# Attention layer and gated graph steps on one core: another start-up, another order of loads, and new ranks for the planner

## The chip, the cores and the metric

The kernel runs on one core of a Trainium2 chip. The time is the device time of one execution in microseconds (us). TensorE multiplies matrices, VectorE (DVE) and ScalarE (ACT) do elementwise work, GpSimd (POOL) does small arithmetic and can issue DMAs, SyncE (SP) issues most DMAs. Each engine works through its own instructions strictly in order, and waits on semaphores for the others.

## The reference

The input x is 16 batches of 1024 nodes by 128 features; adj is a symmetric 0/1 matrix of 1024 by 1024 with a full diagonal. Two layers are computed, each as layernorm(x + layer(x)).

```python
# layer 0: attention over graph edges
h = x @ others_weight
u1, u2 = h @ a1, h @ a2              # a1, a2: the two halves of att_weight
e = u1[:, idx1] + u2[:, idx2]        # pairs of nodes
e = where(e >= 0, e, 0.1 * e)
att = softmax(where(adj > 0, e, -9e15), axis=1)
out = einsum('bik,bkl->bil', att, h) + x @ self_weight

# layer 1: five gated steps
m_in = m_out = einsum('nm,bmd->bnd', adj, h)
av = concatenate([m_in, m_out])
u3 = h @ u3_w.T + u3_b
z = sigmoid(av @ w3_w.T + w3_b + u3)
r = sigmoid(av @ w4_w.T + w4_b + u3)
hv = tanh(av @ w5_w.T + w5_b + (r * h) @ u5_w.T + u5_b)
h = (1 - z) * h + z * hv
```

The pair indices are such that in the first half of the columns a logit depends on two neighbouring nodes of the second index alone, and in the other half on the row alone. So the attention of a batch needs one vector of 1024 logits (u1 + u2 of the same node, exponentiated) spread over all partitions, called pb, and one number for each row, called q.

## The kernel before

**A planner orders everything.** The kernel does not emit instructions as its code runs. Each piece of work is put into a `Plan` (L36 to L134) with its engine, a length in ns, a rank, the tiles that it reads and writes, and the function that emits it. `order()` plays the plan through in model time: whenever an engine is free, the ready piece with the lowest rank whose buffers are free is started. A piece that needs another engine's result becomes ready after a lag (`LAG`, L47: 150 ns after VectorE, 170 after ScalarE, 2400 after a DMA), for TensorE after VectorE or ScalarE with another `CARE` = 400 ns (L45, L125), and lengths on these two are multiplied by 1.1. The order in which the pieces were started becomes the fixed program of each engine. So ranks and model lengths set the order of all work, and nothing of it can change while the kernel runs.

**Ranks.** A step s of batch b has the rank 10 * (b // 2) + 4.2 * s (`rank_of`, L314), layer 0 of a batch has `rank0` (L317), and the table D (L303, L304) holds an offset for every kind of work: m for copying a message bank out, pu and u for the product with u3, pr and pz for the gates, r for the product r * h, pv and hv for the candidate, h for the update, tr for the turn of the new state, o and ln for the end of a batch, l1 to l8 for the parts of layer 0. Batches come in pairs q = b // 2. Pairs are staggered, so that attention of later batches runs beside the gated steps of earlier ones. `LATER` (L29) puts the last batch behind its partner in the last three steps.

**Work on TensorE.** In layer 0, h of a batch (ph, L668), the two attention halves (po, L631 through `product`), the self products (px, L935 and L949, with wsi = self weight + identity). In layer 1, the messages: a state is split into a high and a low part (`split`, L613), and multiplied with the adjacency matrix, in most steps by a scheme with seven instead of eight quarter products (L1130 to L1180), which needs the sums T1 to T4 of quarters of adj (`sums_of_adj`, L499, 16 operations on VectorE). Then per half of a batch the gates: L1199, L1209 twice, L1225, L1226.

**The start.** `early_loads` (L340) issues the first loads: x of batch 0 in two halves, the weights for the logits, adj in eight blocks of 256 rows by 512 columns (`adj_half`; first the four left ones, then the four right ones), the self weight, x of batch 1, then the w, u and bias loads, all of the latter on SyncE. `lands` (L372) tells the planner when each is there. The vector of logit weights is made by a transpose of att to columns (L409), a product with the transposed others_weight (pw, L398), and four small VectorE operations (wv_, L400). Its sum, broadcast over 128 columns (T_ws), is the weight of `spread_` (L744), whose product with x gives the logits of batch 0 on all partitions. `lrelu_` and `exp_` (L747, L753) turn them into pb. `adj_tables` (L473) copies adj into its rounded form, with the count of each row's right half. `z_` (L822) sums each row, `rz_` (L840) makes the reciprocals, `hi_` and `lo_` (L870, L876) scale and split h, and po follows. `ahead` (L444) makes the self products of batches 4 to 7 early (x halves in free r and z buffers, bank ps_ahead, L455) and stores them in DRAM.

**Filler.** `fill_` and `idle_` (L417 to L429) are matmuls and transposes of the identity on TensorE with no use for the result: two fills, and 60 pieces of two transposes at rank 9000, which the planner starts whenever TensorE has nothing else.

Of the kernel before, what the change touches and what calls it, by code (L numbers as in the profile page):

```python
# [9 lines left out]
F32 = mybir.dt.float32  # L10
# [15 lines left out]
LOW, HIGH = -20.0, 100.0  # L26
TINY = 1e-30
PLAIN = {(0, 0), (0, 1), (0, 2), (7, 2), (7, 3), (7, 4)}
LATER = 1.5  # L29
# [3 lines left out]
IDLE = 60  # L33


class Plan:  # L36
# [8 lines left out]
    CARE = 400  # L45
    SAME = {"PE": 0, "DVE": 60, "ACT": 60, "POOL": 60, "SP": 2500, "DMA": 0}
    LAG = {"PE": 250, "DVE": 150, "ACT": 170, "POOL": 200, "SP": 2500, "DMA": 2400}  # L47

    def __init__(self, slots):
        self.slots = dict(slots)  # L50
        self.ops = []
        self.lag = {}
        self.writer, self.readers = {}, {}

# [19 lines left out]
    def order(self):  # L74
# [14 lines left out]
        while events:  # L89
# [13 lines left out]
            while more:  # L103
                more = False
                for engine, queue in ready.items():
# [3 lines left out]
                    while queue:  # L109
# [3 lines left out]
                        if all(free[t[0]] > 0 for t in new):  # L113
# [3 lines left out]
                            started.append(i)  # L117
                            busy[engine] = more = True
# [19 lines left out]
def kernel(  # L138
# [72 lines left out]
    att2 = const.tile([P, 2], F32, tag="att2", name="att2")  # L211
# [3 lines left out]
    bad = const.tile([P, 5], F32, tag="bad", name="bad")  # L215
    flag = const.tile([1, 1], I32, tag="flag", name="flag")

    def exact(pools):
# [84 lines left out]
        D = dict(m=-0.8, pu=1.4, u=0.8, pr=0.8, pz=1.2, r=1.7, pv=1.0, z=1.3, hv=-0.4, h=1.2, tr=1.6, o=6.6, ln=2.9)  # L303
        D.update(out=4.4, l1=-9, l2=-4, l3=-2, l4=-4, l5=-7, l6=-1.5, l7=-1, l8=-2)  # L304

# [8 lines left out]
        def rank_of(b, s):  # L314
            return 10 * (b // 2) + 4.2 * s + (LATER if b == B - 1 and plain(b // 2, s) else 0)

        def rank0(b):  # L317
            return 10 * (b // 2) - 1 * (1 - b % 2) + -1.0 - 6 * (b // 2 == 1)
# [7 lines left out]
        cols = {"wot": slice(0, 128), "ws": slice(128, 256), "w345": slice(256, 1024)}  # L326
# [13 lines left out]
        def early_loads():  # L340
            nc.sync.dma_start(T(x0)[:, HALF:N], x_t[0][:, HALF:N])
            nc.scalar.dma_start(T(x0)[:, 0:HALF], x_t[0][:, 0:HALF])
            nc.sync.dma_start(W("wot"), others_wt)
            nc.scalar.dma_start(T(ws)[0:2, P : 2 * P], att_w.rearrange("(t p) o -> t (p o)", p=P))
            nc.sync.dma_start(*adj_half(0, 0))
            nc.scalar.dma_start(wo[:, 0:P], others_w)
            nc.sync.dma_start(*adj_half(1, 0))
            nc.scalar.dma_start(*adj_half(2, 0))
            nc.sync.dma_start(*adj_half(3, 0))
            for k in range(NC // 2):  # L350
                nc.sync.dma_start(*adj_half(k, 1))
            nc.sync.dma_start(W("ws"), self_w)
            nc.sync.dma_start(T(("xt", 1)), x_t[1])
            for j, w in enumerate((w3_t, w4_t, w5_t)):
                nc.sync.dma_start(
                    W("w345")[:, 256 * j : 256 * (j + 1)].rearrange("p (t e) -> p t e", t=2),
                    w.rearrange("(t p) e -> p t e", p=P),
                )
            nc.sync.dma_start(u3, u3_t)
            nc.sync.dma_start(u5, u5_t)  # L360
            for j, v in enumerate((w3_b, w4_b, w5_b, u3_b, u5_b)):
                nc.sync.dma_start(T(ws)[j : j + 1, 2 * P : 3 * P], v.rearrange("(o p) -> o p", o=1))


        sp(
            6000,
# [5 lines left out]
        def lands(pieces, what):  # L372
            plan.add("DMA", 190 * pieces, -103, lambda: None, writes=what)

        lands(8, [(x0, 0), (x0, 1)])
        lands(1, [(boot, "wot"), (ws, "att")])
        lands(8, [(staged[0][0], 0)])
        lands(1, [(("wo",), 0)])
        for k in range(1, NC // 2):
            lands(8, [(staged[k][0], 0)])  # L380
        for k in range(NC // 2):
            lands(8, [(staged[k][1], 0)])
        lands(9, [(boot, "ws"), (("xt", 1), 0), (("xt", 1), 1)])
        lands(10, [(boot, "late"), (("uw",), 0), (ws, "b")])
# [7 lines left out]
        plan.add("POOL", 2000, -100, constants, writes=[(("ident",), 0), (("ones",), 0)])  # L392


        pw = ("ps", "g", "w")

        def pw_():
            nc.tensor.matmul(T(pw)[:, 0:2], W("wot"), att2, start=True, stop=True)  # L398

        def wv_():  # L400
            nc.vector.tensor_copy(wv, T(pw)[:, 0:2])
            nc.vector.tensor_copy(wo[:, P : P + 2], wv)
            nc.vector.tensor_tensor(wo[:, P + 2 : P + 3], wv[:, 0:1], wv[:, 1:2], ALU.add)
            nc.vector.tensor_copy(T(ws)[:, 0:P], wo[:, P + 2 : P + 3].to_broadcast([P, P]))

        pa = ("ps", "g", "a")
# [4 lines left out]
        pe(150, -101, lambda: column_(pa, slice(P, 2 * P), 2), reads=[(ws, "att"), (("ident",), 0)], writes=[(pa, 0)])  # L411
        dve(160, -101, lambda: nc.vector.tensor_copy(att2, T(pa)[:, 0:2]), reads=[(pa, 0)], writes=[(("att2",), 0)])
        pe(350, -100, pw_, reads=[(boot, "wot"), (("att2",), 0)], writes=[(pw, 0)])
        dve(600, -100, wv_, reads=[(pw, 0), (("wo",), 0)], writes=[(("wo",), 1), (ws, 0)])


# [27 lines left out]
        def ahead():  # L444
            dve(270, -8, self_, reads=[(boot, "ws"), (("ident",), 0)], writes=[(("wsi",), 0)])
            for b in AHEAD:
                d = ("PX", b)
                for e in range(2):
                    bank, px, x = ("ps", "ahead", b, e), ("m", "px", b, e), ("rz"[e], "x", b)
                    hs = slice(e * HALF, (e + 1) * HALF)  # L450
                    sp(450, -89, lambda x=x, b=b, hs=hs: nc.sync.dma_start(T(x), x_t[b][:, hs]), writes=[(x, "sent")], lag=0)
                    plan.add("DMA", 4 * 190, -101, lambda: None, reads=[(x, "sent")], writes=[(x, 0)])
# [5 lines left out]
                    act(A, -5.5, lambda bank=bank, px=px: nc.scalar.copy(T(px), T(bank)), reads=[(bank, 0)], writes=[(px, 0)])  # L458
# [8 lines left out]
        def own_weights():  # L467
            pb_ = ("ps", "g", "b")
            pe(150, -4.6, lambda: column_(pb_, slice(2 * P, 3 * P), 5), reads=[(ws, "b"), (("rz", 0), 1)], writes=[(pb_, 0)])
            dve(160, -4.3, lambda: nc.vector.tensor_copy(bias, T(pb_)[:, 0:5]), reads=[(pb_, 0)], writes=[(("bias",), 0)])  # L470
            dve(1000, -4.2, sums, reads=[(boot, "late"), (("bias",), 0), (("uw",), 0), (("rz", 0), 1)], writes=[(("wm",), 0)])

        def adj_tables(c):  # L473
            st = staged[c // 2]

            def left(copy):
                copy(adj[:, c, 0:HALF], T(st[0])[:, c % 2])

            def right():
                nc.scalar.activation(adj[:, c, HALF:N], T(st[1])[:, c % 2], AF.Identity, accum_out=cnt[:, c : c + 1])  # L480

            if c < 4:
                dve(420, -60, lambda: left(nc.vector.tensor_copy), reads=[(st[0], 0)], writes=[(("A",), c, 0)])
            else:
                act(A, -60, lambda: left(nc.scalar.copy), reads=[(st[0], 0)], writes=[(("A",), c, 0)])
            act(640, -50, right, reads=[(st[1], 0)], writes=[(("A",), c, 1)])
# [12 lines left out]
        def sums_of_adj(c):  # L499
# [17 lines left out]
            for n, (sum_, first) in enumerate(((t1, None), (t3, None), (t2, 0), (t4, 2))):  # L517
                more = [] if first is None else [(("tab",), c, first)]
                dve(V, 1 + c / 4, sum_, reads=[*y, *more], writes=[(("tab",), c, n)])
# [121 lines left out]
        def layer0(b):  # L641

            first = rank0(b) - (60 if b == 0 else 0)
            rank = first + D["l1"]
# [6 lines left out]
            if b in (2, 3):  # L651
                xt = ("hT", "x", b)
            q, zs, rz, hT = ("q", b), ("zs", b), ("rz", b), ("hT", b)
# [7 lines left out]
            for g in range(4):  # L661
# [18 lines left out]
                pe(460, rank, ph_, reads=[(xt, g // 2), (("wo",), 1)], writes=[(ph, 0), (hx, g, "place")])  # L680
# [55 lines left out]
            else:  # L736

                if b == 0:

                    for e in range(2):  # L740
# [14 lines left out]

                        pe(F, rank - 0.1, spread_, reads=[(xt, e), (ws, 0)], writes=[(pp, 0)])
                        dve(2 * V, rank - 0.1, lrelu_, reads=[(pp, 0)], writes=[(pb, e)])
                        act(A, rank - 0.1, exp_, reads=[(pb, e), (("ones",), 0)], writes=[(pb, e)])
# [34 lines left out]

            rank = first + D["l2"]

# [20 lines left out]
            rank = rank0(b) + D["l2"]  # L816
            junk = ("junk", b)
# [19 lines left out]
            for k in range(2 if b == 0 else 1):  # L837
                cs = slice(4 * k, 4 * k + 4) if b == 0 else slice(0, NC)

                def rz_(k=k, cs=cs):  # L840
# [3 lines left out]
                    if b == 0:  # L844
                        least = T(("rstd", "least"))[:, 0, k : k + 1]
                        nc.vector.tensor_reduce(least, w, AX.X, ALU.min)
                        nc.vector.tensor_scalar(bad[:, k : k + 1], least, 0.0, None, ALU.is_le)
                    nc.vector.tensor_scalar(w, w, TINY, None, ALU.max)
                    nc.vector.reciprocal(w, w)
                    nc.vector.tensor_tensor(T(rz)[:, 1, cs], w, T(q)[:, cs], ALU.mult)  # L850

# [6 lines left out]
                    writes=[(rz, k), (("bad",), k), (("rstd", "least"), k)] if b == 0 else [(rz, 0), (rz, 1)],  # L858
                )
            if b == 0:  # L860
                own_weights()
            rank = rank0(b) + D["l3"]
# [28 lines left out]
            rank = rank0(b) + D["l4"]  # L891
# [28 lines left out]
            px = ("xt", b, "px") if b in AHEAD else ("ps", "acc", b, "px")  # L920
            if b in AHEAD:
# [3 lines left out]
                    rank0(b) + D["l3"],  # L925
# [5 lines left out]
            else:  # L931
# [4 lines left out]
                    reads=[(xt, 0), (("wsi",), 0), (yT[1], "p")],  # L936
# [14 lines left out]
            begun = [(hl[1][0], c, 1) for c in range(4)]  # L951
# [21 lines left out]
            for g in range(2):  # L973
                rank = rank0(b) + D["l5"]
# [734 lines left out]
```

## Time and profile before

| | |
|---|---|
| time, median of 3 runs | 1455.69 us |
| lowest and highest | 1454.83 and 1457.84 us |
| span of the profiled execution | 1457.2 us |
| mean granted TensorE clock | 0.995 |
| last matmul starts | 1445.82 us |
| DMA moved | 174.20 MB, mean 120 GB/s |

The profiled execution's own total is not recorded beside its span; the span runs from its first to its last instruction. On the page, busy time is the union of an engine's instructions. PE is TensorE, PEld its weight loads. A row of the timeline gives start, length, engine, line, operation, output and inputs, count, and in brackets the idle time before it with what ended it.

### The profile page before, as it was taken

Reading aid. Unit: us, or ns where it says so; the run is one execution under the profiler, and the core shown is the slowest. Engines: PE = TensorE matmul, PEld = TensorE weight load, DVE = VectorE, ACT = ScalarE, POOL = GpSimd, SP = SyncE. Lnnn points to the kernel's source line nnn. Section 1 sums busy time; section 2 is a strip of 40 time slices with the busy share of each in tenths; the row PEclk is TensorE's granted clock in tenths of the full one; section 3 lists DMA queues with packets and bytes.
Section 4 is the critical chain, followed back from the end, with each engine's and each line's share of the span. In section 5 each row is a group of like instructions: output and inputs, shape, how many; then the busy total and the mean of one; then the engine's idle time right before and its main releaser. Section 6 shows DMA issues by size and latency. Waiting matters only on the chain.

```text
span 1457.2 us, 17798 instructions
## 1 busy us (share of the span) xinstructions
PE 1437.5 (99%) x5020; PEld 901.6 (62%) x5020; DVE 1161.3 (80%) x2753; ACT 897.1 (62%) x1792; POOL 194.8 (13%) x323
## 2 busy tenths in 40 slices
PE   8999999999999999999999999999999999999996
PEld 7766656666666666665666656666666666565663
DVE  5887879888899788878898778886989867866435
ACT  5657565666666666756667566566665666654544
POOL 0311001012110120110201112001210112000201
PEclk9999999999999999999999999999999999999998
DMA  7426134455345543445344553455433544223201
GB/s 252 136 58 210 48 102 139 120 174 160 88 137 146 152 132 103 135 130 145 110 116 116 148 148 96 116 142 170 118 84 99 163 139 122 80 58 87 73 0 31
DMA packets 188048, 174.20 MB, mean 120 GB/s; under 512 B 34255, under 2 KB 137382, under 8 KB 187942
## 3 DMA queue, kind: packets, MB, share of 16 engines
q1 hardware_dynamic: 182306, 156.28, 37.7%
q0 software_dynamic: 4800, 15.73, 3.2%
q8 instruction: 41, 0.67, 0.2%
q10 hardware_dynamic: 836, 0.98, 0.2%
q14 instruction: 65, 0.53, 0.1%
HBM read 95.68 MB, written 77.24 MB: 119 GB/s over the span
## 4 chain that ended last, share of the span: by engine, by line
PE 97%; DMA 2%; DVE 1%; ACT 0%; issue 0%; SPq 0%; POOL 0%; POOLq 0%; DVEq 0%; ACTq 0%
PE ps_acc_a L631 17%; PE ps_g_r L1209 9%; PE ps_g_r L1199 9%; PE gz L1209 9%; PE ps_g_v L1225 9%; PE ps_g_v L1226 9%; PE ps_acc_c L631 9%; PE ps_acc_po L631 8%; PE ps_acc L631 6%; PE gz L631 4%; PE ps_g_ph L668 2%; PE ps_acc_px L935 1%; PE ps_acc_po L949 1%; PE ps_t L581 1%; DMA blk_boot<-in_adj_dram 1%; DMA hT_boot<-in_L_gnn_w_w_dram 1%
## 5 line engine op out<-in xcount | busy, mean ns | idle before, releaser
L1225 PE MATMUL ps_g_v<-m,wm 128*128 128x512 f32 x320 | 163.5, 592 | 0.1
L1226 PE MATMUL ps_g_v<-r,u5h 128*128 128x512 f32 x320 | 163.4, 592 | 0.0
L1209 PE MATMUL ps_g_r<-m,wm 128*128 128x512 f32 x320 | 159.1, 592 | 1.1 <-ACT gz L1202 1.1
L1209 PE MATMUL gz<-m,wm 128*128 128x512 f32 x320 | 158.8, 592 | 0.0
L1199 PE MATMUL ps_g_r<-hT,u 128*128 128x512 f32 x320 | 153.1, 592 | 0.0
L1219 DVE SCALAR_TENSOR_TENSOR r<-r,hT 128x512 f32<-128x512 f32 x160 | 108.7, 685 | 54.0 <-ACT r L1212 53.4
L1212 ACT ACTIVATE r<-ps_g_r,bh 128x512 f32<-128x512 f32 x160 | 109.4, 687 | 63.6 <-PE ps_g_r L1209 61.1
L631 PE MATMUL ps_acc_a<-tab,blk_s 128*128 128x512 f32 x544 | 147.0, 412 | 0.0
L1234 DVE TENSOR_TENSOR hv<-hv,hT 128x512 f32<-128x512 f32 x160 | 109.6, 686 | 45.1 <-ACT hv L1231 44.6
L631 PE MATMUL ps_acc_po<-adj,blk 128*128 128x512 f32 x512 | 138.1, 417 | 0.0
L1212 ACT ACTIVATE z<-gz,bh 128x512 f32<-128x512 f32 x160 | 109.3, 687 | 24.0 <-PE gz L1209 23.2
L631 PEld LDWEIGHTS ps_acc_a<-tab,blk_s 128*128 128x128 f32 x544 | 101.1, 188 | 32.6 <-issue 9.4
L631 PEld LDWEIGHTS ps_acc_po<-adj,blk 128*128 128x128 f32 x512 | 96.2, 189 | 33.6 <-issue 9.6
L1202 ACT COPY gz<-ps_g_r 128x512 f32<-128x512 f32 x160 | 91.1, 572 | 33.2 <-PE ps_g_r L1199 31.7
L1240 DVE SCALAR_TENSOR_TENSOR hT<-hv,hT 128x512 f32<-128x512 f32 x160 | 107.9, 678 | 1.4
L1237 DVE SCALAR_TENSOR_TENSOR hv<-z,hv 128x512 f32<-128x512 f32 x160 | 107.7, 677 | 1.4 <-ACT z L1212 0.5
L1226 PEld LDWEIGHTS ps_g_v<-r,u5h 128*128 128x128 f32 x320 | 60.6, 190 | 76.7 <-issue 64.2
L1209 PEld LDWEIGHTS gz<-m,wm 128*128 128x128 f32 x320 | 60.6, 190 | 76.5 <-issue 76.5
L631 PE MATMUL ps_acc<-adj,blk_h 128*128 128x512 f32 x384 | 101.5, 414 | 0.0
L533 POOL TENSOR_SCALAR rstd_y<-mv_y 128x4 f32<-128x4 f32 x32 | 12.7, 397 | 660.6 <-DVE mv_y L529 660.2
L623 DVE TENSOR_TENSOR blk_s<-G,blk_s 128x512 fp32r<-128x512 f32 x136 | 91.3, 682 | 12.0 <-ACT blk_s L619 11.6
L619 ACT CAST blk_s<-G 128x512 fp32r<-128x512 f32 x136 | 82.1, 618 | 29.1 <-DVE G L1093 26.2
(191 smaller groups left out, 2584.4 us busy)
## 6 DMA issues: line engine op xcount, KB each, us to landing
G<-X SPq DMA_DIRECT2D x140, 256.0 KB
X<-T SPq DMA_DIRECT2D x552, 64.0 KB
yd<-y POOLq DMA_DIRECT2D x32, 256.0 KB, 3.3
D_y<-T_y SPq DMA_DIRECT2D x112, 64.0 KB
F_y<-D_y SPq DMA_DIRECT2D x28, 256.0 KB
X<-y SPq DMA_DIRECT2D x28, 256.0 KB
D_b<-T_b SPq DMA_DIRECT2D x112, 64.0 KB
F_b<-D_b SPq DMA_DIRECT2D x28, 256.0 KB
```

Source lines behind the costliest of these rows:

```text
L623: lambda: nc.vector.tensor_tensor(half(1), src(), half(0), ALU.subtract),
L631: nc.tensor.matmul(T(bank), T(blk)[:, k, c, :], right(c), start=(first and i == 0), stop=(last and i == len(terms) - 1), skip_group_check= ...
L1199: nc.tensor.matmul(T(pr), u3, h(), start=True, stop=True)
L1202: nc.scalar.copy(T(pz), T(pr))
L1209: nc.tensor.matmul(T(p_), wm[:, j, :], T(m), start=False, stop=True, skip_group_check=True)
L1212: nc.scalar.activation(T(t), T(p_), AF.Tanh, bias=bh[:, j : j + 1], scale=0.5 * sg)
L1219: lambda r=r, h=h: nc.vector.scalar_tensor_tensor(T(r), T(r), 1.0, h(), ALU.add, ALU.mult),
L1225: nc.tensor.matmul(T(pv), wm[:, 2, :], T(m), start=True, stop=False)
L1226: nc.tensor.matmul(T(pv), u5h, T(r), start=False, stop=True)
L1234: nc.vector.tensor_tensor(T(hv), T(hv), h(), ALU.subtract)
L1237: nc.vector.scalar_tensor_tensor(T(hv), T(z), 1.0, T(hv), ALU.add, ALU.mult)
L1240: nc.vector.scalar_tensor_tensor(h(), T(hv), 0.5, h(), ALU.mult, ALU.add)
```

## The change

The vectors of logit weights are now made on VectorE, by multiplying others_weight with a broadcast copy of att and summing along the row. The blocks of adj are loaded in row order (left and right of one block of rows after each other). The w, u and bias loads are issued by GpSimd, behind a copy that reads the last block of adj. Of the second half of batch 0's logits, ScalarE makes two exponentials from the bank and VectorE takes the larger. Batch 0's px goes to a gz bank, and neither its px nor its second product waits for the earlier part of the batch. The check for a vanishing row sum moves out of the chain. The ranks of layer 0 have their own entries for batches 0 and 1. Nearly every offset of D, some lags and CARE change, and NUDGE adds a number to the rank of single steps and batches.

```diff
+MOST = math.exp(HIGH - SHIFT)
+LARGE = 0.999e30
-LATER = 1.5
+LATER = 0.75
+NUDGE = {(3, 2): -0.6, (3, 3): 0.3, (0, 1): -0.5, (1, 1): 0.45, (2, 3): -0.2, (3, 1): -1.2, (3, 0): 0.6, (0, 2): 0.25, (2, 2): -0.6, (1, 4): -1.2, (1, 3): 0.3, (0, 3): -0.6, (1, 2): -0.15, (4, 0): -0.1, (2, 0): 1.2, (2, 1): 0.05, (4, 4): -0.3, (2, 4): -0.15, (7, 3): -0.75, (5, 4): 1.2, (4, 3): 1.25, (6, 3): -1.5, (6, 4): -0.6, (8, 2): 0.15, 10: 0.05, (11, 3): -1.2, (11, 4): 0.3, (7, 2): 0.3, (8, 3): -0.6, (12, 3): -0.45, (13, 3): -0.9, (12, 0): 1.15, (10, 3): -0.35, (8, 4): 0.05, (12, 4): -0.3, (12, 1): -0.05, (11, 2): -0.15, 12: -0.05, (13, 4): 1.2, (13, 0): 1.2, (11, 1): 0.05, (12, 2): 0.15, (10, 4): 0.1, (15, 0): -0.6, (14, 2): -0.6}
...
-    CARE = 400
+    CARE = 250
...
-    LAG = {"PE": 250, "DVE": 150, "ACT": 170, "POOL": 200, "SP": 2500, "DMA": 2400}
+    LAG = {"PE": 250, "DVE": 330, "ACT": 80, "POOL": 200, "SP": 2500, "DMA": 3000}
...
-        D = dict(m=-0.8, pu=1.4, u=0.8, pr=0.8, pz=1.2, r=1.7, pv=1.0, z=1.3, hv=-0.4, h=1.2, tr=1.6, o=6.6, ln=2.9)
-        D.update(out=4.4, l1=-9, l2=-4, l3=-2, l4=-4, l5=-7, l6=-1.5, l7=-1, l8=-2)
+        D = dict(m=-0.05, pu=1.4, u=0.95, pr=0.55, pz=0.85, r=0.25, pv=1.05, z=1.3, hv=-0.7, h=1.2, tr=2.55, o=6.35, ln=2.5, out=4.4, l1=-9, l2=-4, l3=-2, l4=-5.5, l5=-7.25)
+        D.update(l6=-1.35, l7=-1, l8=-2, q=10, s=4.2, even=1, base=-1, q1=-6, b1=4, lz=-4, l1_0=-9, l2_0=-4, lz_0=-4, l3_0=-2, l4_0=-4, l5_0=-7, l6_0=-1.5, l7_0=-1, l8_0=-2)
+        D.update(l1_1=-10, l2_1=-9, lz_1=-4, l3_1=-2, l4_1=-4, l5_1=-7, l6_1=-1.5, l7_1=-1, l8_1=-2, tab=8, tabc=1, cl=-5.9, ca=-50, cr=-51, px=-3.5, own=-2, ownw=-4.6)
...
-            return 10 * (b // 2) + 4.2 * s + (LATER if b == B - 1 and plain(b // 2, s) else 0)
+            return D["q"] * (b // 2) + D["s"] * s + NUDGE.get((b, s), 0) + (LATER if b == B - 1 and plain(b // 2, s) else 0)
...
-            return 10 * (b // 2) - 1 * (1 - b % 2) + -1.0 - 6 * (b // 2 == 1)
+            return NUDGE.get(b, 0) + D["q"] * (b // 2) - D["even"] * (1 - b % 2) + D["base"] + D["q1"] * (b // 2 == 1) + D["b1"] * (b == 1)
...
             nc.sync.dma_start(T(x0)[:, HALF:N], x_t[0][:, HALF:N])
             nc.scalar.dma_start(T(x0)[:, 0:HALF], x_t[0][:, 0:HALF])
-            nc.sync.dma_start(W("wot"), others_wt)
-            nc.scalar.dma_start(T(ws)[0:2, P : 2 * P], att_w.rearrange("(t p) o -> t (p o)", p=P))
+            nc.sync.dma_start(wo[:, 0:P], others_w)
+            nc.scalar.dma_start(T(ws)[:, P : 3 * P], att_w.rearrange("k o -> o k").to_broadcast([P, 2 * P]))
             nc.sync.dma_start(*adj_half(0, 0))
-            nc.scalar.dma_start(wo[:, 0:P], others_w)
-            nc.sync.dma_start(*adj_half(1, 0))
-            nc.scalar.dma_start(*adj_half(2, 0))
-            nc.sync.dma_start(*adj_half(3, 0))
-            for k in range(NC // 2):
-                nc.sync.dma_start(*adj_half(k, 1))
+            nc.scalar.dma_start(*adj_half(1, 0))
+            nc.sync.dma_start(*adj_half(0, 1))
+            nc.scalar.dma_start(*adj_half(1, 1))
             nc.sync.dma_start(W("ws"), self_w)
+            for k in range(2, NC // 2):
+                for e in range(2):
+                    nc.sync.dma_start(*adj_half(k, e))
             nc.sync.dma_start(T(("xt", 1)), x_t[1])
...
+        lands(4700, [(x0, 0), (x0, 1)])
+        lands(400, [(("wo",), 0), (ws, "att")])
+        for ns, k, e in ((3600, 0, 0), (1400, 1, 0), (1000, 0, 1), (1400, 1, 1), (1600, 2, 0), (1400, 2, 1), (1400, 3, 0), (1400, 3, 1)):
+            lands(ns, [(staged[k][e], 0), *([(boot, "ws")] if (k, e) == (2, 0) else [])])
+        lands(1400, [(("xt", 1), 0), (("xt", 1), 1)])
+
+        def late_loads():
+            nc.gpsimd.tensor_copy(mark, T(staged[3][1])[0:1, 0, 0:1])
...
+            nc.gpsimd.dma_start(u3, u3_t)
+            nc.gpsimd.dma_start(u5, u5_t)
+            for j, v in enumerate((w3_b, w4_b, w5_b, u3_b, u5_b)):
+                nc.gpsimd.dma_start(T(ws)[j : j + 1, 3 * P : 4 * P], v.rearrange("(o p) -> o p", o=1))
...
+        def wv_():
+            for two in range(2):
+                nc.vector.scalar_tensor_tensor(
+                    T(("look", "wv"))[:, two * P : (two + 1) * P],
+                    wo[:, 0:P],
+                    1.0,
+                    T(ws)[:, (1 + two) * P : (2 + two) * P],
+                    ALU.mult,
+                    ALU.mult,
+                    accum_out=wv[:, two : two + 1],
+                )
+            nc.vector.tensor_tensor(
+                T(ws)[:, 0:P], wv[:, 0:1].to_broadcast([P, P]), wv[:, 1:2].to_broadcast([P, P]), ALU.add
+            )
...
-                    sp(450, -89, lambda x=x, b=b, hs=hs: nc.sync.dma_start(T(x), x_t[b][:, hs]), writes=[(x, "sent")], lag=0)
+                    sp(450, -91, lambda x=x, b=b, hs=hs: nc.sync.dma_start(T(x), x_t[b][:, hs]), writes=[(x, "sent")], lag=0)
...
-                    act(A, -5.5, lambda bank=bank, px=px: nc.scalar.copy(T(px), T(bank)), reads=[(bank, 0)], writes=[(px, 0)])
+                    act(A, D["px"], lambda bank=bank, px=px: nc.scalar.copy(T(px), T(bank)), reads=[(bank, 0)], writes=[(px, 0)])
...
-                dve(420, -60, lambda: left(nc.vector.tensor_copy), reads=[(st[0], 0)], writes=[(("A",), c, 0)])
+                dve(420, D["cl"], lambda: left(nc.vector.tensor_copy), reads=[(st[0], 0)], writes=[(("A",), c, 0)])
...
-                dve(V, 1 + c / 4, sum_, reads=[*y, *more], writes=[(("tab",), c, n)])
+                dve(V, D["tab"] + D["tabc"] * c, sum_, reads=[*y, *more], writes=[(("tab",), c, n)])
...
+                        def exps_(pp=pp, hs=hs):
+                            nc.scalar.activation(T(pb)[:, hs], T(pp), AF.Exp, bias=shift, scale=1.0)
+                            nc.scalar.activation(T(junk), T(pp), AF.Exp, bias=shift, scale=ALPHA)
+
+                        def larger_(hs=hs):
+                            nc.vector.scalar_tensor_tensor(T(pb)[:, hs], T(pb)[:, hs], MOST, T(junk), ALU.min, ALU.max)
...
-            px = ("xt", b, "px") if b in AHEAD else ("ps", "acc", b, "px")
+            px = ("xt", b, "px") if b in AHEAD else ("gz", b, "px") if b == 0 else ("ps", "acc", b, "px")
...
-                    reads=[(xt, 0), (("wsi",), 0), (yT[1], "p")],
+                    reads=[(xt, 0), (("wsi",), 0), *([(yT[1], "p")] if b else [])],
...
-            begun = [(hl[1][0], c, 1) for c in range(4)]
+            begun = [(hl[1][0], c, 1) for c in range(4)] if b else []
```

## The prediction

> **What bounds the kernel now.** I read the page's busy table first, then its slices, the chain of waits, and who TensorE waited for; after that the timeline of TensorE for the first 60 us and the last 20 us, with the windows beside it.
>
> ```profile
> span 1457.2 us, 17798 instructions
> ...
> PE 1437.5 (99%) x5020; PEld 901.6 (62%) x5020; DVE 1161.3 (80%) x2753; ACT 897.1 (62%) x1792; POOL 194.8 (13%) x323
> ...
> PE   8999999999999999999999999999999999999996
> ...
> PE 97%; DMA 2%; DVE 1%; ACT 0%; issue 0%; SPq 0%; POOL 0%; POOLq 0%; DVEq 0%; ACTq 0%
> ```
>
> TensorE is busy for all but 19.7 us, and the chain is TensorE for 97%. A change of ranks can win nothing in the middle; only the first and last slices show a gap. The list of TensorE's waits gives nearly all of it:
>
> ```profile
> PE ps_t L581 <- DVE hT L1240: 2.8, 2, 1.5
> PE ps_ahead L455 <- DMA r_x<-in_x_dram: 2.2, 1, 2.2
> PE gz_fill L423 <- POOL ones L389: 1.4, 1, 1.4
> PE ps_g_r L1209 <- ACT gz L1202: 1.1, 1, 1.1
> PE ps_p L745 <- DVE T_ws L404: 0.4, 1, 0.4
> PE ps_g_ph L668 <- ACT hx L678: 0.3, 1, 0.3
> PE ps_g_ph L668 <- DMA xt<-in_x_dram: 0.2, 1, 0.2
> ```
>
> By place: head 1.35 + 0.43 + 0.22 + 2.24 = 4.24 us; middle 0.35 + 1.14 = 1.49 (at 117 and 142 us); end 1.31 + 1.47, and from the last matmul (1446.1) to 1457.2 another 11.1, so 13.9.
>
> Busy is not useful, though. The timeline of TensorE shows what fills the head:
>
> ```profile
> 13.41 4.53 PE L419 MATMUL ps_idle<-ident 128*128 128x128 f32 x40
> ...
> 22.92 3.44 PE L419 MATMUL ps_idle<-ident 128*128 128x128 f32 x30
> ...
> 28.75 1.10 PE L455 MATMUL ps_ahead<-r_x,wsi 128*128 128x512 f32 x2 [2.24 <-DMA r_x<-in_x_dram]
> ...
> 30.12 3.42 PE L766 MATMUL ps_p<-ident,u 128*128 128x128 f32 x16
> ```
>
> The ps_idle rows are filler: their six runs add to 120 transposes of 0.109 us, 13.1 us, after 3.6 us of gz_fill. Before 28.75 us only the two sets of 16 ph matmuls, two spreads and the pairs are work, 6.4 us. From 28.75 us the engine is saturated with work. The last row is a second loss: 16 matmuls take 3.42 us that at 0.109 would take 1.75. The windows show why:
>
> ```profile
> 31.00:32.00 1.00, 1.00 (x6) 1.00 (x6) 1.00 (x6) 0.19 (x2) 0.00 (x0) 0.50 0.86 303
> 32.00:33.00 1.00, 1.00 (x7) 1.00 (x6) 0.58 (x3) 0.46 (x1) 0.00 (x0) 0.50 0.69 264
> ```
>
> Column seven, the granted clock, is 0.50. With the next group (3.98 in the chain for 16 of po, 3.73 elsewhere) that is 1.67 + 0.25 = 1.9 us lost to the clock after the 2.24 us gap. The gap itself comes from SyncE, which issued the five biases and two whole x before r_x:
>
> ```profile
> 17.89 3.27 SPq L362 DMA_DIRECT2D T_ws<-in_L_gnn_w_b_dram  x3
> 21.37 0.68 SPq L362 DMA_DIRECT2D T_ws<-in_L_gnn_u_b_dram  x2
> 22.23 0.83 SPq L656 DMA_DIRECT2D hT_x<-in_x_dram  x2
> 23.11 0.42 SPq L451 DMA_DIRECT2D r_x<-in_x_dram  x1
> ```
>
> Over 19 to 23 us the DMA rate falls from 390 to below 30 GB/s: nothing was queued.
>
> **What the Trainium skill says.** "TensorE: Matmul & The Clock Gate", section "What's actually happening", says the array's clock halves after a window of about 3.4 us with too little activity. The trace agrees in kind: half clock from 30.3 to 33.7 us, although the gap was 2.24 us, not a full window. "DMA: Bandwidth & Descriptors", section "Issuing engines are not separate DMA queues", says that another issuing engine saves only sequencer time. The trace agrees that this is what is at stake: SyncE's sequencer was the late one while the 16 engines stood empty. So moving ten small loads to GpSimd should bring r_x forward, not make bytes faster.
>
> **The change part by part.** The sum is over TensorE's time of the profiled execution: 19.7 idle + 1437.5 busy.
>
> *Loads.* Ten DMAs (three w, u3, u5, five biases) leave SyncE; the x halves of the ahead batches go (-91) before the two whole x (-90). r_x then follows x of batch 1 directly. That x landed at 21.06 us (the ph wait); the bytes ahead of it barely change (others_wt out, 64 KB; a broadcast att in, 128 KB). At 0.39 MB/us a 256 KB half takes 0.67 us, so r_x lands near 21.7, not 28.6. The wait of 2.24 us goes, and with it the slow clock: **-2.2 and -1.9**. What is late next is batch 1's x itself, at 20 to 21 us. Filler reaches it: 1.35 + 3.6 + 13.1 + ps_p 1.8 + ph 1.8 + pairs 0.4 + the two px of batch 0, now freed of yT, 1.7 = 23.8 us.
> GpSimd's ten issues start after the last adj block; at 0.54 to 0.79 us for one (its yd rows) they end near 27 us. Queued behind them is only the layernorm power, first needed at 47.45, and their reader wm at some 80 us: hidden by 20 us. If GpSimd were four times slower, the first y of batch 0 would wait.
>
> *Logit vectors.* Gone: a transpose (0.26), pw (0.28), five small VectorE copies. New: two multiply-accumulates 128x128, bound from the nearest rows, 0.34 (L878) + 0.08 (accumulator) = 0.42 each, and one 128x128 add 0.28 (L432): 1.1 us after wo and att land (att was there at 5.49, wo below 6.3). I take T_ws at 7.3 (6.7 to 8.2) against 9.75. TensorE loses two matmuls while the 120 fillers stay: **-0.4**.
>
> *Batch 0's softmax.* Of the second half ScalarE takes two exponentials (2 x 0.72) and VectorE one max (0.69) instead of two operations; the halves run beside each other. From 7.3: spreads to 9.2, ScalarE 9.2 to 11.3, pb complete at 11.4 against 15.28. In row order the first four chunks' counts are done near 16, so their rz moves from 22.6 to about 16.5; the last block lands near 19.5, two rights of 0.84 and 0.9 of small operations put the second rz at 22.1 against 24.38. ScalarE's 4.0 us stop behind ps_ahead (25.9 to 29.9), with eight hi casts behind it, goes. These let batch 0's products follow x of batch 1 without a gap; they are no term of their own, because **the filler count is fixed at 120**: an earlier chain cannot save more than true idle time, unless leftover fillers move to the drain. I book **-0.5** (0 to -2.5) for that.
>
> *New idle in the head.* The 0.43 and 0.22 waits were from a plan of landing times; the new plan states other ones (last x at 19.7). If it lands at 21 again, TensorE waits about 1. I take 1.0 (0 to 2.5) against 0.65: **+0.35**, short of a new slow clock.
>
> *Ramp.* VectorE was 90% busy from 50 to 125 us. The 16 table sums (0.69 each, 11 us) go from rank 1 to 8 and later; the tables are first read at 158 us (ps_acc_c), so that load is spread. Batch 1 stands 4 units behind batch 0, so one hides the other. The 1.49 us of middle waits I halve (0 to 4 possible): **-0.75**.
>
> *All other ranks.* The middle has no idle to win, so at most a loss. ScalarE-to-TensorE allowance falls from 170 + 400 to 80 + 250 ns, VectorE's rises from 550 to 580. The trace's real handover at the end is 0.05 us (L1202 to L1209), so 330 still covers: **+0.4**.
>
> *End.* Ranks there change (LATER 1.5 to 0.75, tr 1.6 to 2.55): batch 14's transposes stand at 86.8 + 2.55 = 89.35, behind batch 15's first pu, 88.95, before the second, 89.75. Between -0.9 (they fill a gap) and +1.9 (batch 14's add and statistics run ahead of batch 15's on VectorE); I take 0.
>
> Sum: -2.2 - 1.9 - 0.4 - 0.5 + 0.35 - 0.75 + 0.4 = **-5.0 us**. Span 1457.2 to 1452.2. The profiled execution's total is not shown, and its span lies 1.5 above the median of the runs, so I subtract from the median: 1455.7 - 5.0 = **1450.7**.
>
> **Rivals.** (1) *The gain is given back in the ramp.* For it: VectorE at 94% in 100:125, and both middle waits lie there. Against: the table sums leave. Idle of 4 us between 60 and 150: 1454.5. (2) *The steady state stalls, slower.* There are 160 half-gates with three handovers to TensorE each (gz copy, m copy, r), 480 in all. If the new order puts the reader too soon in one of eight, at 0.15 us, that is 60 x 0.15 = 9 us: 1459.7. It decides from 5.0/480 = 10 ns on average. For it: every order is new and the allowance is smaller. Against: before shows only two such stalls, none after 143 us. (3) *More than forecast.* Fillers go to the drain (-2) and the middle waits vanish (-0.75), the end gains 0.5: 1447.5. (4) The moved loads don't help because r_x waits for free r and z buffers or a full queue: then 2.2 and 1.9 stay, 1454.8; against it, six halves went out without such a wait before. It goes with (1).
>
> **How the numbers follow.** Forecast 0.47, (1) with (4) 0.21, (2) 0.17, (3) 0.15. A measurement here tells 0.2%, 2.9 us, so faster is below 1452.8 and slower above 1458.6. Faster: 0.45 + 0.15 + 0.05 = 0.65; same 0.18; slower 0.17. The range for 8 in 10 is 1447 to 1460; the likeliest case alone gives 1448.5 to 1453.
>
> **What would show it.** Right: no wait of ps_ahead for r_x, granted clock 1.0 from 10 us to 1440, spreads of batch 0 near 7.5 us, first po of batch 0 before 26 us instead of 33.2, TensorE's idle near 17 us, its busy time down by some 2. Wrong: waits on ACT gz, ACT m or DVE r between 150 and 1400 us, a half clock in the head, or a drain over 16 us from the last pv. An idle time below 15 us, or fillers after 1440 us, would say that I valued the filler wrongly.

## The result

| | before | changed |
|---|---|---|
| median, 20 runs each | 1456.43 us | 1455.11 us |
| lowest and highest | 1454.22 and 1459.66 | 1454.15 and 1458.06 |
| ratio, 95% interval | | 0.9991 (0.9984 to 0.9998) |
| span of the profiled execution | 1457.2 us | 1453.5 us |

The gain is 1.3 us, 0.09%: no change by the bound of 0.2%, though the interval (0.3 to 2.3 us) lies below before. Between the two profiled executions it is 3.7 us.

The page of the changed kernel, its first lines:

```profile
span 1453.5 us, 17779 instructions
...
PE 1435.8 (99%) x5017; PEld 899.7 (62%) x5017; DVE 1159.7 (80%) x2752; ACT 897.4 (62%) x1793; POOL 193.5 (13%) x334
...
PE   9999999999999999999999999999999999999995
```

TensorE is busy for 1.7 us less and idle for 17.7 us instead of 19.7. Who it waited for (releaser, then total us, times, longest):

```profile
PE ps_t L598 <- DVE hT L1275: 4.4, 2, 3.6
PE gz_fill L440 <- POOL ones L403: 1.4, 1, 1.4
PE ps_acc L648 <- ACT blk_h L636: 0.8, 1, 0.8
PE ps_acc L648 <- DVE blk_h L640: 0.2, 1, 0.2
PE ps_t_b L598 <- ACT y L565: 0.2, 1, 0.2
```

The waits for r_x, for T_ws and for x of batch 1 are gone, and the granted clock is 1.00 throughout the start. The middle has 1.2 us here against 1.49. The end has grown: ps_t waits 4.4 us for the new state instead of 2.8. The timeline of TensorE, start and end:

```profile
4.93 4.16 PE L436 MATMUL ps_idle<-ident 128*128 128x128 f32 x30
8.92 1.88 PE L767 MATMUL ps_p<-xt,T_ws 128*128 128x512 f32 x4
...
12.43 4.75 PE L436 MATMUL ps_idle<-ident 128*128 128x128 f32 x42
...
19.89 2.56 PE L436 MATMUL ps_idle<-ident 128*128 128x128 f32 x22
22.29 1.95 PE L690 MATMUL ps_g_ph<-wo,xt 128*128 128x131 f32 x16
24.08 1.91 PE L436 MATMUL ps_idle<-ident 128*128 128x128 f32 x16
25.82 1.02 PE L472 MATMUL ps_ahead<-r_x,wsi 128*128 128x512 f32 x2
...
30.23 3.97 PE L648 MATMUL ps_acc_po<-adj,blk 128*128 128x512 f32 x16
```

```profile
1432.48 1.02 PE L1261 MATMUL ps_g_v<-r,u5h 128*128 128x512 f32 x2
...
1437.81 1.02 PE L1261 MATMUL ps_g_v<-r,u5h 128*128 128x512 f32 x2
1442.46 0.63 PE L598 MATMUL ps_t<-ident,hT 128*128 128x128 f32 x4 [3.64 <-DVE hT L1275]
```

All 120 filler transposes still run before the first po: 30 + 42 + 6 + 22 + 16 + 2 + 2. There is no wait before the spread at 8.92 us, although its weight is made by an operation that starts at 7.63 and takes 0.29: filler stood in front of it. At the end the two halves of batch 15 have their last pv 5.3 us apart (1432.48 and 1437.81), so TensorE has nothing left while the second half finishes. Before they were 1.7 apart:

```profile
1439.27 1.02 PE L1226 MATMUL ps_g_v<-r,u5h 128*128 128x512 f32 x2
...
1440.98 1.02 PE L1226 MATMUL ps_g_v<-r,u5h 128*128 128x512 f32 x2
```

One thing that I had not foreseen shows on ScalarE:

```profile
10.89 1.28 ACT L779 ACT_TABLE_LOAD   x1 [10.89 <-PE ps_p L767]
12.19 0.69 ACT L779 ACTIVATE pb<-ps_p,shift 128x512 f32<-128x512 f32 x1
```

Before, the table load came ahead of anything else:

```profile
2.65 1.28 ACT L477 ACT_TABLE_LOAD   x1 [2.65 <-issue]
```

Now ScalarE's first operation is an exponential that waits for the spread, and the load waits with it: 1.28 us in batch 0's chain.

### The profile page after: what moved, and what is told of

It is laid out like the page before. It is cut to its first block, busy times and chain, and to the rows that moved or that the text cites. A ratio compares the mean times of both kernels' runs of the same rounds, so it can differ in the third digit from the quotient of the medians.

```text
span 1453.5 us, 17779 instructions
## 1 busy us (share of the span) xinstructions
PE 1435.8 (99%) x5017; PEld 899.7 (62%) x5017; DVE 1159.7 (80%) x2752; ACT 897.4 (62%) x1793; POOL 193.5 (13%) x334
## 5 line engine op out<-in xcount | busy, mean ns | idle before, releaser
L1247 ACT ACTIVATE z<-gz,bh 128x512 f32<-128x512 f32 x160 | 109.6, 688 | 18.3 <-PE gz L1244 17.7
L606 DVE STREAM_TRANSPOSE T<-hT 128x512 f32<-128x512 f32 x138 | 95.4, 699 | 3.5 <-issue 1.8
L648 PE MATMUL ps_acc<-adj,blk_h 128*128 128x512 f32 x384 | 95.4, 402 | 1.0 <-ACT blk_h L636 0.8
L1260 PEld LDWEIGHTS ps_g_v<-m,wm 128*128 128x128 f32 x320 | 60.0, 190 | 57.6 <-issue 51.7
```

What stands on the lines that cost most here:

```text
L606: nc.vector.transpose(T(t).rearrange("p (b c i) -> p b c i", b=4, c=4), turned(src()))
L648: nc.tensor.matmul(T(bank), T(blk)[:, k, c, :], right(c), start=(first and i == 0), stop=(last and i == len(terms) - 1), skip_group_check= ...
L1247: nc.scalar.activation(T(t), T(p_), AF.Tanh, bias=bh[:, j : j + 1], scale=0.5 * sg)
L1260: nc.tensor.matmul(T(pv), wm[:, 2, :], T(m), start=True, stop=False)
```

## The experiments

Three questions: is the start's gain real in most executions; do the new ranks give something back; and does the filler bound the start. Each table row gives this kernel's median, the median of before on the same chip, and the ratio.

### Before once more, and each part planned on its own

`a1_before_again` is the kernel before, unedited.

> The kernel before, once more. Theory A (the profile that I read was of an execution slower than most: its half clock, 1.9 us, comes with some executions only): the ratio to before is 1.0000 within 0.0005, and this profile has the wait of ps_ahead for r_x near 2.2 us but a span 1 to 3 us below 1457.2 and no or a shorter stretch of granted clock 0.5 near 30 us. Theory B (the gain of the start was real in every execution and was given back elsewhere in the changed kernel): the wait and the half clock are both here again, span near 1457.

`a2_loads_only`: the loads and their order moved, the planner told so.

```diff
-            for j, w in enumerate((w3_t, w4_t, w5_t)):
-                nc.sync.dma_start(
...
+        plan.add("POOL", 11000, -80, late_loads, reads=[(staged[3][1], 0)],
+            writes=[(boot, "late"), (("uw",), 0), (ws, "b")], lag=2500)
...
-                    sp(450, -89, lambda x=x, b=b, hs=hs: nc.sync.dma_start(T(x), x_t[b][:, hs]), writes=[(x, "sent")], lag=0)
+                    sp(450, -91, lambda x=x, b=b, hs=hs: nc.sync.dma_start(T(x), x_t[b][:, hs]), writes=[(x, "sent")], lag=0)
```

> Before with one part: the w, u and bias loads issued by GpSimd behind the last adj block, and the x halves of the ahead batches before the two whole x. Theory A: the wait for r_x goes, 2.2 us at most, so 1454.2 to 1455.5 against a before of 1456.4. Theory B: wait and clock go, 4 us, so near 1452.4. Rival: fillers take the place of the wait, no change (1456).

`a3_start_only` is the changed kernel with old step ranks, lags and CARE; `a4_ranks_only` is the mirror image, the start of before with the new ones.

```diff
-LATER = 0.75
+LATER = 1.5
...
-NUDGE = {(3, 2): -0.6, ...
+NUDGE = {}
...
-    CARE = 250
+    CARE = 400
...
-    LAG = {"PE": 250, "DVE": 330, "ACT": 80, "POOL": 200, "SP": 2500, "DMA": 3000}
+    LAG = {"PE": 250, "DVE": 150, "ACT": 170, "POOL": 200, "SP": 2500, "DMA": 2400}
...
-        D = dict(m=-0.05, pu=1.4, u=0.95, pr=0.55, ...
+        D = dict(m=-0.8, pu=1.4, u=0.8, pr=0.8, ...
...
```

> The changed kernel with the ranks of the gated steps, LATER, the lags and CARE of before, and no NUDGE: the new start alone. Theory A: the new ranks cost or bring little, 1455 as the changed kernel. Theory B: without the new ranks the start's whole gain shows, 1452 to 1453.

> Before with the step ranks, LATER, lags, CARE and NUDGE of the change, and the start of before. Theory A: within 1 us of before, 1455.5 to 1457.5. Theory B: slower than before by the 2 to 4 us that the ranks give back, 1458.5 to 1460.5.

| | median | before | ratio (95%) |
|---|---|---|---|
| a1_before_again | 1456.49 | 1455.76 | 1.0002 (0.9994 to 1.0010) |
| a2_loads_only | 1465.85 | 1455.76 | 1.0061 (1.0048 to 1.0074) |
| a3_start_only | 1464.21 | 1455.76 | 1.0049 (1.0036 to 1.0062) |
| a4_ranks_only | 1463.13 | 1455.76 | 1.0043 (1.0027 to 1.0059) |

All three parts are slower than before by 7 to 10 us, and slower than the whole; neither theory had that. The waits of TensorE in a3_start_only say where it comes from:

```profile
PE ps_g_r L1244 <- ACT gz L1237: 3.8, 3, 2.7
PE ps_t L598 <- DVE hT L1275: 2.8, 2, 1.5
PE ps_acc_a L648 <- ACT m L1186: 1.7, 1, 1.7
PE gz_fill L440 <- POOL ones L403: 1.4, 1, 1.4
PE ps_t_b L598 <- ACT y L565: 1.0, 1, 1.0
```

Against the changed kernel, idle time is 22.5 us instead of 17.7, and busy time 1440.8 instead of 1435.8, of which 1.6 us and 1.4 us are lost to the clock in 100:120 and 50:60, after such waits. So each plan made anew for the same work brings stalls of several us in all, between 45 and 1300 us; I read that as ranks that are fitted to their start. The parts of the change can't be added up by planning each on its own, and the next experiments keep the emission order of everything else.

a1 alone does not decide between the theories. The wait and the half clock (column seven) are both there again, as in B, with 1.7 us lost to the clock; but this profiled execution took 1458.12 us against a median of 1456.49, so it too is slower than most, as in A:

```profile
PE ps_ahead L455 <- DMA r_x<-in_x_dram: 2.4, 1, 2.4
```

```profile
29.00:30.00 1.00, 1.00 (x5) 1.00 (x6) 0.90 (x6) 0.67 (x3) 0.00 (x0) 0.50 0.68 205
30.00:31.00 1.00, 1.00 (x7) 1.00 (x6) 1.00 (x5) 0.11 (x1) 0.00 (x0) 0.50 0.97 363
31.00:32.00 1.00, 1.00 (x7) 1.00 (x6) 0.23 (x1) 0.48 (x1) 0.00 (x0) 0.50 0.16 59
```

The profile that the prediction was made from is of this kind too: its span is 1457.2 us, and over the 95 executions of before that ran beside these experiments the median span is 1453.8. I had measured the start from an execution that was 3.4 us above the typical one.

### The start alone, with all other orders kept

`f1_loads_same_order`: all ten small loads on GpSimd, emitted after its constants; nothing planned anew.

```diff
-            for j, w in enumerate((w3_t, w4_t, w5_t)):
-                nc.sync.dma_start(
...
             nc.gpsimd.memset(mhalf, -0.5)
+            nc.gpsimd.tensor_copy(mark, T(staged[3][1])[0:1, 0, 0:1])
+            for j, w in enumerate((w3_t, w4_t, w5_t)):
+                nc.gpsimd.dma_start(
...
+            nc.gpsimd.dma_start(u3, u3_t)
+            nc.gpsimd.dma_start(u5, u5_t)
+            for j, v in enumerate((w3_b, w4_b, w5_b, u3_b, u5_b)):
+                nc.gpsimd.dma_start(T(ws)[j : j + 1, 2 * P : 3 * P], v.rearrange("(o p) -> o p", o=1))
```

> Before, with the order of every other instruction kept as it was: the w, u and bias loads leave SyncE for GpSimd (behind the last adj block); nothing is planned anew. Theory C (the start of before really costs wait and clock, and each new plan costs or brings several us of its own in the middle): the wait of ps_ahead for r_x is below 0.5 us, no granted clock below 1 near 30 us, and the time falls by 2.2 us and up to 1.9 more, 1452 to 1454.5, with no stall after 150 us. Theory A (half of the executions of before have no such loss): the highest times go and the lowest stay, median near 1455. Rival: something else holds TensorE at once, no change.

1458.56 against 1456.37, ratio 1.0017 (1.0007 to 1.0027): slower. The rival held in kind: something else stopped TensorE at once. It had forecast no change, though. TensorE's wait, and GpSimd's last bias loads in the timeline:

```profile
PE ps_g_b L410 <- DMA T_ws<-in_L_gnn_u_b_dram: 2.6, 1, 2.6
```

```profile
24.47 0.49 POOL L391 DMA_DIRECT2D T_ws<-in_L_gnn_u_b_dram  x1 [1.36 <-DMA hT_boot<-in_L_gnn_w_w_dram]
25.28 0.49 POOL L391 DMA_DIRECT2D T_ws<-in_L_gnn_u_b_dram  x1 [0.32 <-DMA hT_boot<-in_L_gnn_w_w_dram]
```

r_x was in time, but the transpose of the biases, next in TensorE's order, waited as long for the last bias, and a half clock of 6.8 us followed (28.0 to 34.8), twice as long as in before. In the changed kernel that transpose stands at 40.93 us, so there the late biases cost nothing.

`g4_loads_biases_kept` is f1 without the last two lines of its diff: the biases stay on SyncE. `g1_before_warm` leaves the loads and puts 20 more transposes in front of the wait.

```diff
-            pe(2 * TR, 9000, idle_, reads=[(("ident",), 0)], writes=[(("ps", "idle"), 0)])
+            pe(2 * TR, 9000, idle_ if i < IDLE - 1 else (lambda: [idle_() for _ in range(11)]), reads=...
```

> Before, all other orders kept: the three w, u3 and u5 are issued by GpSimd, the five biases stay on SyncE, so neither the biases nor r_x come late. Theory C: the wait for r_x falls from 2.2 to below 0.5 us, no half clock, time 2 to 4 us below before. Theory A: 1.5 to 2.5 below. Rival (the time of the start returns as waits further on): wait and half clock gone in the profile, the time within 1 us of before, and new waits between 40 and 160 us.

> Before, with 20 more filler transposes (2.2 us) ahead of the first ps_ahead, all orders kept: the wait for r_x stays as time, but TensorE has no gap there. Theory A (the half clock comes with some executions): median 0.5 to 1.2 us below before, highest times lower, lowest times unchanged; clock 1.00 over 30:35 in the profile. Theory C (half clock in every execution): 1.4 to 1.9 us below before. Rival: the filler delays the work behind it, slower by up to 2.

| | median | before | ratio (95%) |
|---|---|---|---|
| g4_loads_biases_kept | 1453.93 | 1455.69 | 0.9985 (0.9979 to 0.9992) |
| g1_before_warm | 1456.90 | 1455.69 | 1.0007 (1.0000 to 1.0014) |

The start of g4_loads_biases_kept in TensorE's timeline:

```profile
24.91 0.22 PE L411 MATMUL ps_g_b<-ident,T_ws 5*128 5x5 f32 x1
25.47 1.10 PE L457 MATMUL ps_ahead<-r_x,wsi 128*128 128x512 f32 x2 [0.34 <-DVE bias L472]
26.50 0.42 PE L786 MATMUL ps_pairs<-u,ident 128*64 128x4 f32 x8
26.85 2.05 PE L768 MATMUL ps_p<-ident,u 128*128 128x128 f32 x16
28.65 3.98 PE L633 MATMUL ps_acc_po<-adj,blk 128*128 128x512 f32 x16
```

Wait and half clock are gone (the 16 matmuls into ps_p take 2.05 us, not 3.42), and nothing new stands in the middle. Yet the time falls by 1.8 us, within theory A's 1.5 to 2.5 and short of the 4.1 us of the profile. In g1 the profile has no clock below 1.00 at the start either, with 0.9 us of new idle in 60:70, and the median rises by 1.2 us: its rival held. If the half clock were in a typical execution of before, filling the gap would have gained up to 1.9 us; with a gap typically shorter than 2.2 us, the filler costs instead.

No trace shows a typical execution of before, but two measurements tell something of it. The first is the mean granted clock of each execution. It is 0.995 or less in both profiles of before, and in 23 of its 108 executions, counting a1's own (their median is 1458.3 us); in the other 85 it is 0.996 or more (1455.6 us). In all 9 executions of f1 it is 0.995 or less, in all 42 of g1 and g4 0.996 or more. That fits a half clock near 30 us in about one execution of before in five; it is a hint and no count, because the mean also holds the idle end of the kernel. The second is an estimate of the wait. In before the first po starts here:

```profile
33.19 4.32 PE L631 MATMUL ps_acc_po<-adj,blk 128*128 128x512 f32 x16
```

From there to the end of the span is 1424.0 us, and in the profiles of a1, f1, g1 and g4, which keep this order, 1423.3 to 1424.2. Taken from the median span of 1453.8 us, that puts the first po of a typical execution near 30 us: about 3 us ahead of the profiled one, and only 1 to 2 us behind the 28.65 of g4.

### The filler and the table load

All five are the changed kernel with its order kept. `f2_table_early` emits one small exponential after the constants; the others leave filler out.

```diff
             nc.gpsimd.memset(mhalf, -0.5)
+            nc.scalar.activation(warm, ones, AF.Exp)
...
-            pe(2 * TR, 9000, idle_, reads=...
+            pe(2 * TR, 9000, idle_ if i % 2 else (lambda: None), reads=...
```

f3 has the second edit alone, f4 both, g2 both with `i % 3 == 0`, g3 both with no pair kept.

> The changed kernel with one tiny exponential on ScalarE right after the constants, so that the table load of 1.28 us stands before the first wait and not at 10.9 us behind the spread; all other orders kept. Theory F (fillers fix the head: 120 of them run before the first po whatever the chain does): pb 1.2 us earlier, TensorE's head and the time unchanged within 0.3 us. Theory G (ScalarE's chain bounds the head): 1.0 to 1.3 us faster.

> The changed kernel with every second pair of filler transposes left out (60 remain), all other orders kept. Theory F: TensorE comes to the spread of batch 0 near 8 instead of 8.9 us and to the first po up to 2 us earlier, 1 to 2 us faster. Theory G: the 6.5 us of filler turn into waits of the same length, time unchanged, or slower by up to 2 if the clock drops to half in one of the gaps.

> Both of these in the changed kernel. Theory F with G (each hides the other's gain): 2 to 3.5 us faster than the changed kernel, 1451.5 to 1453. Theory F alone: as the half filler; theory G alone: as the early table.

> The changed kernel with the early table load and one filler pair in three left (40 transposes). If fillers still delay the head after half of them is gone: up to 1 us faster than with half of them, 1451.3 to 1452.3. If the waits bound it now: equal to it, 1452.3, and with a half clock in a gap slower, 1453 to 1454.

> The changed kernel with the early table load and no idle transposes at all (the two fills stay). If the clock needs them: granted clock 0.5 over several us between 5 and 30 us, the first po later than with half of the fillers, 1453 to 1456. If not: as with half of them, 1452.3.

| | filler | first po | median | before | ratio (95%) |
|---|---|---|---|---|---|
| changed kernel | 120 | 30.23 us | 1455.11 | 1456.43 | 0.9991 (0.9984 to 0.9998) |
| f2_table_early | 120 | 30.10 | 1454.16 | 1456.37 | 0.9989 (0.9980 to 0.9997) |
| f3_half_filler | 60 | 26.70 | 1454.10 | 1456.37 | 0.9991 (0.9982 to 0.9999) |
| f4_half_filler_table | 60 | 26.16 | 1452.30 | 1456.37 | 0.9978 (0.9969 to 0.9987) |
| g2_third_filler_table | 40 | 26.19 | 1450.57 | 1455.69 | 0.9965 (0.9951 to 0.9978) |
| g3_no_filler_table | 0 | 26.86 | 1450.59 | 1455.69 | 0.9963 (0.9949 to 0.9976) |

With all filler the early table changes nothing: theory F. Half the filler left out changes nothing either, against theory F's 1 to 2 us; both together (f4) are 1.8 us below each alone, on the same chip: each hides the other's gain. With a third left, the head is bound by real waits. TensorE's timeline of g2 and, below it, of g3:

```profile
7.80 1.98 PE L769 MATMUL ps_p<-xt,T_ws 128*128 128x512 f32 x4 [1.88 <-DVE T_ws L425]
...
19.38 2.02 PE L692 MATMUL ps_g_ph<-wo,xt 128*128 128x131 f32 x16 [1.32 <-ACT adj L499]
...
26.19 3.98 PE L650 MATMUL ps_acc_po<-adj,blk 128*128 128x512 f32 x16
```

```profile
8.10 3.78 PE L769 MATMUL ps_p<-xt,T_ws 128*128 128x512 f32 x4 [2.97 <-DVE T_ws L425]
11.67 3.10 PE L692 MATMUL ps_g_ph<-wo,xt 128*128 128x131 f32 x16
```

The first po of g2 comes 4.0 us earlier than in the changed kernel, and by the ratios to before its time is 3.8 us lower (the medians, from different chips, differ by 4.5). g3 pays for the missing filler with slower matmuls: the four matmuls of the spread take 3.78 us, not 1.98, although the granted clock reads 1.00 there, and from 17.5 to 20.8 us that clock is 0.50 (column seven has the means of these windows):

```profile
10.00:20.00 10.00, 7.87 (x31) 5.04 (x30) 8.61 (x30) 7.99 (x23) 1.65 (x3) 0.87 1.05 388
20.00:25.00 5.00, 4.82 (x30) 2.98 (x28) 4.17 (x22) 5.00 (x17) 4.02 (x7) 0.92 1.05 384
```

But its first po is only 0.7 us later and its time the same: what the filler does for the clock is worth little here, its place in the order costs. f3 doesn't fit so well: its first po is 3.5 us earlier in the profile, and only 0.5 us behind f4's, but its ratio equals the changed kernel's. Its profiled execution is the lowest of its 13 (1453.28), with a new wait of 1.5 us at 140:160 even so; why the others stand higher isn't shown. g2_third_filler_table beats both kernels: 5.1 us below before, and its interval does not touch the changed kernel's. It carries the early table load as well, so its gain is that of both edits.

## Why the prediction came out as it did

I forecast -5.0 us and measured -1.3. The time lies in the stated range, 1447 to 1460, and outside the likeliest case's own, 1448.5 to 1453. That it lies in the range is owed to the range's width, which holds no change at all as well as a gain of 8.7 us; of the outcomes I gave 0.65 to faster and 0.18 to same, and same came. By its terms, in us:

| term | booked | in the two profiles |
|---|---|---|
| wait for r_x | -2.2 | -2.24 |
| slow clock, and two matmuls fewer | -1.9 - 0.4 | -1.7 (TensorE's busy time) |
| other waits of the head | +0.35 | -0.65 |
| middle and ranks | -0.75 + 0.4 | -0.1 |
| filler that leaves the head | -0.5 | 0 |
| end | 0 | +1.0 |
| sum | -5.0 | -3.7 |

**The mis-sized term.** "The wait of 2.24 us goes, and with it the slow clock: -2.2 and -1.9." Both go, as said. But I took them from one profiled execution, and the step "so I subtract from the median" moved them to a median that did not contain them in full. With the order kept, g4 measured -1.8 us (-3.1 to -1.2 by its interval) for wait and clock together, and by the recorded clocks perhaps one execution in five had the half clock. The clock was a little too large even for the profile: I took 1.75 us for 16 matmuls at full clock, where g4 takes 2.05, and the windows from 30.6 to 33.9 us give 1.7 us lost, not 1.9. The sign was in front of me: I wrote that the span lay 1.5 above the median of the runs, and went on as if it were a harmless offset. A span above the total of another execution means that this execution had losses that the other did not.

**The end.** "I take 0." Idle of TensorE after 1400 us is 13.9 in before, 13.7 in a1 and 13.9 in g4 with the old ranks; 14.8 in the changed kernel, 14.9 in f2 and 15.0 in g2 with the new ones: +1.0. My bounds (-0.9 to +1.9) held it, but I reasoned only from where batch 14's work stands, and what happened is that the two halves of batch 15 drifted 5.3 us apart. Most of that is TensorE's new order: the first gate of each half stands 4.7 us from the other's (1.8 in before).

```profile
1428.61 1.02 PE L1244 MATMUL ps_g_r<-m,wm 128*128 128x512 f32 x2
...
1433.34 1.02 PE L1244 MATMUL ps_g_r<-m,wm 128*128 128x512 f32 x2
```

VectorE adds to it: ScalarE has the second half's r at 1435.1 us, and its product waits until 1436.3 behind the first half's update. The cause that I named for the upper bound, adds and statistics ahead of batch 15's work on VectorE, is there as well, with 0.6 us: the last candidate is ready at 1439.6 us, and VectorE comes to it at 1440.2.

**The filler.** That 120 transposes fix the head was right, and g2 shows the size of it: 3.8 us, with the table load moved as well. I booked -0.5 in the hope that some would leave the head; none did. The chain of batch 0 was also later than I worked out: pb at 14.1 instead of 11.4. The broadcast att landed at 7.1, where I had taken the 5.49 of before's small load of att (and wo below 6.3); filler stood before the spread (about 1 us); and the table load took 1.28. The first po, "before 26 us", came at 30.2. With full filler the table load cost nothing, as f2 shows.

**The ranks.** "The middle has no idle to win, so at most a loss", booked at 0.4, was right for this plan and wrong as a way to price one. a2, a3 and a4 lost 7 to 10 us with other pairs of start and ranks. That the changed plan's middle is as clean as the old one's had to be known from the plan, not from TensorE's share of busy time.

**GpSimd's queue.** I named wm, needed at some 80 us, as the first reader behind it. In the old order it was the transpose of the biases at 26.3, and f1 shows what that would have cost: +0.17%. The new plan moved that transpose to 40.93 us, which I had not seen to be needed.

Of the rivals, (1) with (4), at 1454.5 to 1454.8, is nearest in time, but neither mechanism occurred: the ramp has 1.2 us of waits, and r_x was not late. (2) did not occur in the changed kernel, and of (3) nothing: no filler went to the drain, and the end lost.

About half of the 1.3 us lies outside the span. Total minus span is 2.20 in before (95 runs) and 1.54 in the changed kernel (20 runs), in median; with the loads moved alone it is 1.8 to 2.0. What runs there is not in the trace, and this stays open.

## What to carry to other kernels

Before a loss in a profile is booked against a median, compare that execution's time with the median: a stall and the slow clock after it can belong to the profiled execution more than to the typical one. Where an engine that looks saturated runs filler by a fixed count, the filler is a floor under every gain ahead of it, so thin it in the same step: here neither half the filler nor the early table load gained anything alone. Where a planner orders the program, test an edit with the order of everything else kept; planned anew, the same work can lose several times what the edit is worth (10 us against 1.8 here).

## What was not expected of the hardware

- A single gap of 2.2 to 2.6 us on TensorE was followed by a granted clock of 0.50, for about 3.4 us in before and a1 and for 6.8 us in f1. Gaps of 1.88 and 1.32 us in g2 were followed by none. The length of one gap does not settle it: in a3 three gaps of 1.04, 0.32 and 0.22 us between 45 and 50 us were followed by half clock from 49.4 to 52.9, and in g3 gaps of 1.16 and 0.97 us by half clock from 17.5.
- ScalarE's table load of 1.28 us ran at 2.65 us when its first operation was a copy that waited for a load, and at 10.89 us when it was an exponential that waited for TensorE; with a small exponential in front its wait was gone from the chain.
- GpSimd took from 18.1 to 25.8 us to issue ten small loads (f1), with two stops for earlier ones to land; the last bias was there at 28.3 us.
